# Rows of a batch turned for the queries: by a trip to DRAM and VectorE's 32x32 transposes, instead of TensorE

## The chip, the cores and the metric

The kernel runs on one core of a Trainium2 chip. A core has engines that each take their own instructions in order: TensorE (PE; its weight loads are shown apart as PEld), VectorE (DVE), ScalarE (ACT), GpSimd (POOL) and SyncE (SP), which here only issues DMAs. They wait for each other through semaphores. The metric is the device time of one execution in microseconds (us); it is given as a median of runs.

## The reference

One decoder layer in float32 over 16 sequences of 256 tokens with 256 channels, in three stages, each with a residual and a layer norm:

```python
x = _layernorm(x + _L0_attn_ref(x, w_fc, w_proj, ln_g, ln_b))        # squared-relu "attention" on fixed keys
x = _layernorm(x + _L0_xattn_ref(x, ctx, ctx, frac, Wq, bq, ...))    # 16 heads of 16, 256 keys
x = _layernorm(x + _L0_ffn_ref(x, gate_W, gate_b, wi_W, ...))        # top-1 of 8 LoRA experts
```

The change lies in the cross-attention of the second stage, in how its queries are made:

```python
Q = query @ Wq.T + bq ; K = key @ Wk.T + bk ; V = value @ Wv.T + bv
logits = einsum('bhqd,bhkd->bhqk', Q, K) * scale
D = clip(frac[:, None, :] - frac[:, :, None], -0.2, 0.2)
attn = gamma * logits + delta * (ap * max(D, 0) + an * min(D, 0))
out = softmax(attn) @ V @ Wo.T + bo
```

## The kernel before, in words

All instructions are put in an order by hand; no planner moves them, and each engine runs its share of them in that order.

The first stage runs over 8 blocks of 512 tokens (two batches each). It leaves normed rows in `hid`, a tile of 128 partitions (tokens) x 32 x 256 channels; `norm_out` writes a row block there (ScalarE, L245, then a GpSimd addition of `bo`, L413).

The second stage runs over 64 groups: group n is batch n // 4 and four of its heads. In the loop over n (L1068), group n's scores are made by TensorE (`logits`, L649) on top of a bias that ScalarE has put into the four PSUM banks (`positive`, L640); VectorE adds the other part of the bias and takes maxima (`maxima`, L664); GpSimd and VectorE subtract them (L679); one group later TensorE transposes the result (`Group.turned`, L689), ScalarE takes exponentials (L696), and two groups later TensorE multiplies with the values (`attend`, L705). Between these lie pieces for other batches, given by `pieces(n)` (L727): for n = 4b the queries of batch b+1 (L471), for 4b+1 the output projection of batch b-2 (L601), for 4b+2 the keys of batch b+1 (L497), for 4b+3 its values (L519), and then the small piece `ahead.turned()` for batch b+2. From group 15 on the third stage's blocks (L884, L896, L914) are woven in.

`Batch.turned` (L453) is the piece that the change rewrites. `hid` has tokens on partitions, and the query projection needs channels on partitions. So TensorE transposes the four 128x128 parts of a batch's rows into one PSUM tile (L458), and ScalarE copies it to `xT` (L465). `queries` then multiplies `wq` with `xT`. Batch 0 is turned in the last block of the first stage, batch 1 in group 0, and batch b+2 at the end of group 4b+3.

All DMAs of the second stage are issued by SP, in order. For one batch these are, with the group in which they stand: in group 4b+1 `gather` (L561 `sums`, then eight L569 `v`) for batch b-1; in 4b+2 the reciprocals' trip to DRAM (L579 `rows<-inv`), the eight DMAs that put batch b+1's keys in place (L513, `kM`: first four for heads of groups 4b+4 and 4b+6, then four for the other two) and the eight that spread the reciprocals (L587, `invs`); in 4b+3 loads of a later batch (L438 `cT` and L449, L451 or L442). The division (L594, `divide`) by `invs` is done on VectorE in group 4b+4.

`tile_b()` hands out PSUM tiles in the second stage from three banks in turn. `biases` (L139), in the second block of the first stage, subtracts from `bq` the product of `wq` with the vector `bo` that is added to the rows; it turns `bo` to columns with two TensorE transposes.

Of the kernel before, what the change touches and what calls it, by code (L numbers as in the profile page):

```python
# [14 lines left out]
P = 128  # L15
# [7 lines left out]
def tile_decoder_layer(ctx: ExitStack, tc: tile.TileContext, a: dict, out: bass.AP):  # L23
# [79 lines left out]
    gateb = const.tile([P, 4, E], FP, name="gateb")  # L103
    loraB = const.tile([P, F], FP, name="loraB")

    def load_cross():
        load = nc.sync.dma_start
        for t, n in ((vv, "vv"), (wk, "wkT"), (wv, "wvT"), (wq, "wqT")):
            load(out=t, in_=a[n].rearrange("(c p) f -> p c f", p=P))
        for t, n in ((bq, "bq"), (bk, "bk"), (fcol, "frac_cols")):  # L110
            load(out=t, in_=a[n])
        for t, n in (
            (bo, "bo"), (apos, "alpha_pos"), (aneg, "alpha_neg"), (gamma, "gamma"),
            (delta, "delta"),
        ):
            load(out=t, in_=a[n].to_broadcast(list(t.shape)))

        wo_view = a["woT"].rearrange("(o g i d) f -> i g d o f", o=CC, g=4, i=2)
        bv_view = a["bv"].rearrange("x (o g i d) -> i g d (x o)", o=CC, g=4, i=2)
        for i in range(2):  # L120
            for g in range(4):
                rows = slice(64 * i + 16 * g, 64 * i + 16 * g + 16)
                load(out=wo[rows], in_=wo_view[i, g])
                load(out=bvc[rows], in_=bv_view[i, g])
# [14 lines left out]
    def biases():  # L139


        spread = small.tile([P, CC, P], FP, tag="spread", bufs=1, name="spread")
        nc.vector.tensor_copy(spread, bvc.unsqueeze(2).to_broadcast([P, CC, P]))
        yield
        ps = tile_b()
        for c in range(CC):
            nc.tensor.matmul(
                ps[:, 0:C], lhsT=spread[:, c, :], rhs=wo[:, c, :], start=(c == 0), stop=(c == CC - 1)
            )
        nc.vector.tensor_tensor(bo, bo, ps[:, 0:C], ALU.add)  # L150
        yield
        ps = tile_b()
        for c in range(CC):
            nc.tensor.transpose(ps[:, c * P : (c + 1) * P], bo[:, c * P : (c + 1) * P], ident)
        columns = small.tile([P, CC, P], FP, tag="spread", bufs=1, name="columns")
        nc.vector.tensor_copy(columns.rearrange("p c f -> p (c f)"), ps[:, 0:C])
        yield
        ps = tile_b()
        for o in range(CC):
            for c in range(CC):  # L160
                nc.tensor.matmul(
                    ps[:, o * P : (o + 1) * P],
                    lhsT=wq[:, c, o * P : (o + 1) * P],
                    rhs=columns[:, c, :],
                    start=(c == 0),
                    stop=(c == CC - 1),
                )
        for o in range(CC):
            nc.vector.tensor_tensor(
                bq[:, o : o + 1], bq[:, o : o + 1], ps[:, o * P : o * P + 1], ALU.subtract  # L170
            )
        nc.vector.tensor_scalar(bq_s, bq, qscale, None, ALU.mult)
        yield
# [247 lines left out]
    if True:  # L421
# [8 lines left out]
        class Batch:  # L430
# [15 lines left out]
            def reload(self):  # L446
# [3 lines left out]
                self.dpos = p2.tile([P, 2, S], FP, tag="dpos", name="dpos")  # L450
                nc.sync.dma_start(out=self.dpos, in_=self.away["dpos"])  # L451

            def turned(self):  # L453
                b = self.b
                ps = tile_b()
                for c in range(CC):
                    for j in range(2):
                        nc.tensor.transpose(  # L458
                            ps[:, c * S + j * P : c * S + (j + 1) * P],
                            hid[:, 2 * b + j, c * P : (c + 1) * P],  # L460
                            ident,
                        )
                yield
                self.xT = p2.tile([P, CC, S], FP, tag="xT", bufs=1, name="xT")
                nc.scalar.copy(self.xT.rearrange("p c t -> p (c t)"), ps)  # L465

            def queries(self, vector=False):
                ps = tile_b()
# [258 lines left out]
        def pieces(n):  # L727

            b, og = divmod(n, 4)
            ahead, nxt, last, older = (  # L730
                batches[b + d] if 0 <= b + d < B else None for d in (2, 1, -1, -2)
            )
            if og == 0:
                return nxt and nxt.queries(n > 16 and n % 8 == 0), None, []
            later = nxt if nxt and nxt.b >= MADE else None
            if og == 1:
                return older and older.project(), None, [later and (lambda: later.clip("dneg"))]
            if og == 2:
                return nxt and nxt.keys(), None, [later and (lambda: later.clip("dpos"))]
            more = [ahead and ahead.load]  # L740
            if ahead:
                more.append(ahead.reload if ahead.b < MADE else ahead.fractions)
            return nxt and nxt.vals(), ahead and ahead.turned(), more
# [205 lines left out]
    with tc.manual_schedule():  # L949
# [23 lines left out]
        for tb in range(NB):  # L973
            now = rows_in[tb]
            steps = [[] for _ in range(8)]

            mv = small.tile([P, 8, 2], FP, tag="mv8", bufs=2, name="mv8")
            if tb in (0, 1, NB - 1):
                nc.vector.memset(mv, 0.0)

            if tb > 1:
                last = rows_in[tb - 2]
                last.mv = mv[:, 4:8]
                for jj in range(2):
                    steps[1 + jj].append(lambda jj=jj: last.measure_out(jj))
                for j in range(4 if tb + 1 == NB else 1):
                    steps[7 - j // 2].append(
                        lambda j=j, tb=tb: last.norm_out(by[tb], 4 + j, j, nc.gpsimd)
                    )
            if tb > 2:  # L990
                older = rows_in[tb - 3]
                for j in range(1, 4):
                    steps[j].append(
                        lambda j=j, tb=tb: older.norm_out(by[tb - 1], 4 + j, j, nc.gpsimd)
                    )
            turning = []
            if tb + 1 < NB:
                nxt = rows_in[tb + 1]
                nxt.mv = mv[:, 0:4]
                if tb:  # L1000
                    steps[0].append(nxt.load)
                for jj in range(2):
                    steps[3 + jj].append(lambda jj=jj: nxt.measure(jj))
                steps[6].append(lambda tb=tb: nxt.norm_in(by[tb]))
                turning.append(lambda: nxt.turn_in(0))
                if tb:
                    turning.append(rows_in[tb - 1].turn_rows)
                turning.append(lambda: nxt.turn_in(1))
            if tb + 1 < NB or tb > 1:
                steps[5].append(lambda tb=tb, mv=mv: scale(tb, mv))  # L1010
            if tb == 0:
                steps[0] += [load_cross]
                steps[2] += [load_ffn]
            if tb == 1:
                steps[0].append(scales)
                steps[4].append(clips[0][0].fractions)
                output = biases()
                for m in range(4):
                    steps[m + 2].append(lambda: next(output))
            for k, ((at, m), (batch, which)) in enumerate(zip(slots, clips)):  # L1020
                if at == tb:
                    if which == "dneg" and k + 2 < len(clips):
                        steps[m].append(clips[k + 2][0].fractions)
                    steps[m].append(lambda batch=batch, which=which: batch.clip(which))
            if tb + 2 == NB:
                steps[3].append(first.load)
                steps[5].append(batches[1].load)
            if tb + 1 == NB:
                steps[4] += [lambda: groups[0].negative(3)]
                for m, together in ((4, early[:2]), (7, early[2:3])):  # L1030
                    steps[m] += [lambda p=piece: step(p) for piece in together * 2]
            for m in range(8):
                c, n2 = divmod(m, 4)
                coming = []
                for n in (2 * n2, 2 * n2 + 1):
                    coming.append((now, c, n, now.scores(c, n)))
                for block, c, n, pr in behind:
                    block.values(c, n, pr)
                    if n == 7:
                        block.keep(c)  # L1040
                behind = coming
                for piece in steps[m]:
                    piece()
            for piece in turning:
                piece()
# [283 lines left out]
```

## Time and profile before

| | |
|---|---|
| time, median of 3 runs (lowest to highest) | 899.78 us (899.75 to 899.96) |
| span of the profiled execution, first to last instruction | 898.3 us |
| time of the profiled execution beyond its span | not recorded; the median stands 1.48 us above the span |
| mean granted TensorE clock | 0.998 |
| busy: TensorE / VectorE / ScalarE / GpSimd | 887.4 / 713.1 / 567.3 / 398.5 us |
| DMA queue of SP and its share of the 16 DMA engines | 43520 packets, 35.52 MB, 14.5% |
| first stage ends, second begins | about 254 us |

How to read it: an engine's busy share is a mean over stages with different limits. "idle <-X" behind a row names what ended the engine's idle time before it. In a timeline, the first two columns are start and duration in us. A start-to-start distance tells more of TensorE's use than a duration does, since successive matmuls overlap. DMA rows on SP (SPq) show the issue, not the transfer.

### The profile page before, as it was taken

Reading aid. Unit: us, or ns where it says so; the run is one execution under the profiler, and the core shown is the slowest. Engines: PE = TensorE matmul, PEld = TensorE weight load, DVE = VectorE, ACT = ScalarE, POOL = GpSimd, SP = SyncE. Lnnn points to the kernel's source line nnn. Section 1 sums busy time; section 2 is a strip of 40 time slices with the busy share of each in tenths; the row PEclk is TensorE's granted clock in tenths of the full one; section 3 lists DMA queues with packets and bytes.
Section 4 is the critical chain, followed back from the end, with each engine's and each line's share of the span. In section 5 each row is a group of like instructions: output and inputs, shape, how many; then the busy total and the mean of one; then the engine's idle time right before and its main releaser. Section 6 shows DMA issues by size and latency. Waiting matters only on the chain.

```text
span 898.3 us, 19061 instructions
## 1 busy us (share of the span) xinstructions
PE 887.4 (99%) x6940; PEld 560.8 (62%) x6940; DVE 713.1 (79%) x1986; ACT 567.3 (63%) x951; POOL 398.5 (44%) x385
## 2 busy tenths in 40 slices
PE   8999999999999999999999999999999999999997
PEld 4334444444466777577668757766875786586555
DVE  6879899988779999778777877877798787778344
ACT  5766777777787888376656836666684665556111
POOL 1100223422489998435534644563464456344010
PEclk9999999999999999999999999999999999999999
DMA  5501110110001222011111102011110201111001
GB/s 140 154 1 42 53 42 26 30 49 1 14 1 55 70 69 57 14 42 23 34 49 39 47 14 67 20 37 45 43 48 14 66 20 37 43 28 43 23 2 46
DMA packets 44190, 37.01 MB, mean 41 GB/s; under 512 B 14912, under 2 KB 40000, under 8 KB 44096
## 3 DMA queue, kind: packets, MB, share of 16 engines
q1 hardware_dynamic: 43520, 35.52, 14.5%
q8 instruction: 55, 0.90, 0.4%
q14 instruction: 39, 0.32, 0.1%
q10 hardware_dynamic: 576, 0.26, 0.1%
HBM read 21.07 MB, written 6.03 MB: 30 GB/s over the span
## 4 chain that ended last, share of the span: by engine, by line
PE 97%; DVE 1%; ACT 1%; issue 0%; POOL 0%; DVEq 0%; ACTq 0%; POOLq 0%
PE ps_b L689 13%; PE ps_a L339 13%; PE ps_v L358 12%; PE ps_l L884 12%; PE ps_l L649 8%; PE ps_b L914 7%; PE ps_v L705 7%; PE ps_v L914 5%; PE ps_b L601 3%; PE ps_b L497 3%; PE ps_b L471 3%; PE ps_b L519 3%; PE ps_l L896 2%; PE ps_b L811 1%; PE ps_b L458 1%; PE ps_b L796 1%
## 5 line engine op out<-in xcount | busy, mean ns | idle before, releaser
L628 POOL TENSOR_SCALAR neg<-dneg,aneg,delta 128x512 f32<-128x512 f32 x217 | 182.9, 854 | 181.8 <-PE ps_b L689 127.4
L664 DVE CUSTOM_DVE_ANT_0 neg<-ps_l,neg 128x256 f32<-128x256 f32 x512 | 181.5, 420 | 26.5 <-PE ps_l L649 22.6
L640 ACT ACTIVATE ps_l<-dpos,apos_d 128x512 f32<-128x512 f32 x256 | 172.9, 687 | 40.3 <-DVE mx L664 35.6
L696 ACT ACTIVATE pT<-ps_b 128x512 f32<-128x512 f32 x256 | 142.4, 591 | 59.3 <-PE ps_b L689 57.2
L348 DVE TENSOR_TENSOR pr<-pr 128x1024 f32<-128x1024 f32 x128 | 153.9, 1243 | 30.2 <-ACT pr L347 29.8
L347 ACT ACTIVATE pr<-ps_a 128x1024 f32<-128x1024 f32 x128 | 124.9, 1025 | 52.9 <-PE ps_a L339 52.5
L689 PE MATMUL ps_b<-ident,neg 128*128 128x128 f32 x1024 | 138.5, 277 | 2.0 <-ACT pT L696 1.8
L689 PEld LDWEIGHTS ps_b<-ident,neg 128*128 128x128 f32 x1024 | 113.6, 141 | 35.9 <-issue 12.4
L679 POOL TENSOR_TENSOR neg<-neg,mx 128x1024 f32<-128x1024 f32 x65 | 124.2, 1911 | 18.2 <-DVE mx L664 17.0
L339 PE MATMUL ps_a<-xnT,kT 64*64 64x512 f32 x1024 | 124.6, 593 | 1.0 <-ACT xnT L324 0.4
L358 PE MATMUL ps_v<-pr,vv 64*64 64x512 f32 x1024 | 122.7, 589 | 0.0
L884 PE MATMUL ps_l<-xt,wi 128*128 128x512 f32 x248 | 111.5, 595 | 0.0
L679 DVE TENSOR_TENSOR neg<-neg,mx 128x1024 f32<-128x1024 f32 x63 | 99.2, 1575 | 0.6
L413 POOL TENSOR_TENSOR hid<-hid,bo 128x256 f32<-128x256 f32 x32 | 43.7, 1367 | 105.3 <-ACT hid L245 86.5
L358 PEld LDWEIGHTS ps_v<-pr,vv 64*64 64x64 f32 x1024 | 45.2, 133 | 64.4 <-issue 54.5
L339 PEld LDWEIGHTS ps_a<-xnT,kT 64*64 64x64 f32 x1024 | 42.0, 133 | 65.2 <-issue 52.7
L649 PE MATMUL ps_l<-kM,qT 32*128 32x256 f32 x1024 | 75.9, 401 | 0.0
L884 PEld LDWEIGHTS ps_l<-xt,wi 128*128 128x128 f32 x248 | 45.3, 190 | 49.0 <-issue 44.4
L373 POOL TENSOR_TENSOR xt<-xt,half 128x512 f32<-128x512 f32 x15 | 19.1, 1273 | 120.3 <-ACT half L372 120.3
L914 PE MATMUL ps_b<-wof,hT 128*128 128x256 f32 x304 | 68.4, 380 | 0.0
L705 PE MATMUL ps_v<-pT,vaug 128*32 128x256 f32 x1024 | 66.4, 384 | 0.0
L907 DVE TENSOR_SCALAR hT<-ps_l,wib 128x512 f32<-128x512 f32 x43 | 29.8, 746 | 43.9 <-PE ps_l L896 43.9
(131 smaller groups left out, 1087.3 us busy)
## 6 DMA issues: line engine op xcount, KB each, us to landing
cT<-in_ctxT SPq DMA_DIRECT2D x16, 256.0 KB
kM<-keys SPq DMA_DIRECT2D x128, 32.0 KB
v<-raw SPq DMA_DIRECT2D x128, 32.0 KB
invs<-rows SPq DMA_DIRECT2D x128, 32.0 KB
x<-in_x SPq DMA_DIRECT2D x7, 512.0 KB
out<-x SPq DMA_DIRECT2D x7, 512.0 KB
frow<-in_frac SPq DMA_DIRECT2D x16, 128.0 KB
wi<-in_wiT SPq DMA_DIRECT2D x1, 1024.0 KB
```

Of the source, the lines that this page charges most:

```text
L339: nc.tensor.matmul(sc[64 * k : 64 * k + 64, h, :], lhsT=kT[64 * h : 64 * h + 64, q, hf * P + 64 * k : hf * P + 64 * k + 64], rhs=self.xnT[ ...
L348: nc.vector.tensor_tensor(pr, pr, pr, ALU.mult)
L358: nc.tensor.matmul(self.acc[k][64 * h : 64 * h + 64, :], lhsT=vv[64 * k : 64 * k + 64, hf, 64 * q : 64 * q + 64], rhs=pr[64 * k : 64 * k + ...
L628: nc.gpsimd.tensor_scalar(self.neg[:, g], self.batch.dneg, aneg[:, h : h + 1], delta, ALU.mult, ALU.mult,)
L640: nc.scalar.activation(banks[g], self.batch.dpos.rearrange("p j k -> p (j k)"), AF.Copy, scale=apos_d[:, h : h + 1],)
L649: nc.tensor.matmul(banks[g][:, j * S : (j + 1) * S], lhsT=self.batch.qT[rows, self.o, j * P : (j + 1) * P], rhs=self.batch.kM[rows, self.i ...
L664: nc.vector.tensor_tensor_reduce(out=self.t[:, g, j, :], in0=banks[g][:, j * S : (j + 1) * S], in1=self.neg[:, g, j, :], scale=1.0, scalar ...
L679: eng.tensor_tensor(rows, rows, top.to_broadcast([P, 4, S]), ALU.subtract)
L689: nc.tensor.transpose(ps[:, k * S + j * P : k * S + (j + 1) * P], self.t[:, g, j, k * P : (k + 1) * P], ident,)
L696: nc.scalar.activation(self.pT[:, g, :], self.ps[g], AF.Exp)
L884: nc.tensor.matmul(self.banks[g], lhsT=wi[:, c, f * P : (f + 1) * P], rhs=self.xT[:, c, :], start=(c == 0), stop=False,)
L914: nc.tensor.matmul(ps[:, 0:C], lhsT=self.hT[f][:, j * P : (j + 1) * P], rhs=wof[:, f, :], start=(f == 0), stop=(f == FC - 1),)
```

## The change

Three edits.

First, a new piece `Batch.regroup`, which issues five DMAs on SP. One stores a batch's 256 rows of 256 channels from `hid` to a DRAM tile. Four load them into `z`: partition 32q + r gets, of rows r, 32 + r, 64 + r ..., the 64 channels from 64q on, in pieces of 256 bytes. The piece stands at the end of group 4b+1 for batch b+2, after `gather` and before the reciprocals' store; for batches 0 and 1 in the seventh block of the first stage.

Second, `Batch.turned` has no TensorE or ScalarE work: after an empty first step, one VectorE transpose in blocks of 32x32 makes `xT` out of `z`, at the place where ScalarE's copy stood. With that, channel 64q + 32c + s lies on partition 32q + s, chunk c, instead of partition p and chunk c for channel 128c + p.

Third, the query weights are laid out in that order of channels (four DMAs in place of one), and `biases` brings `bo` into that order with one more VectorE copy (128x256).

```diff
+    def blocked(rows):
+        return rows.rearrange("p (q c s) -> p c q s", q=4, c=CC)
+
+    def load_blocked(t, name):
+        view = a[name].rearrange("(q c s) f -> q s c f", q=4, c=CC)
+        for q in range(4):
+            nc.sync.dma_start(out=t[32 * q : 32 * q + 32, :, 0 : view.shape[3]], in_=view[q])
+
     def load_cross():
         load = nc.sync.dma_start
-        for t, n in ((vv, "vv"), (wk, "wkT"), (wv, "wvT"), (wq, "wqT")):
+        for t, n in ((vv, "vv"), (wk, "wkT"), (wv, "wvT")):
             load(out=t, in_=a[n].rearrange("(c p) f -> p c f", p=P))
+        load_blocked(wq, "wqT")
...
         nc.vector.tensor_tensor(bo, bo, ps[:, 0:C], ALU.add)
+        mixed = small.tile([P, CC, P], FP, tag="spread", bufs=1, name="mixed")
+        nc.vector.tensor_copy(mixed.rearrange("p c (q s) -> p c q s", q=4), blocked(bo))
         yield
         ps = tile_b()
         for c in range(CC):
-            nc.tensor.transpose(ps[:, c * P : (c + 1) * P], bo[:, c * P : (c + 1) * P], ident)
+            nc.tensor.transpose(ps[:, c * P : (c + 1) * P], mixed[:, c], ident)
...
+            def regroup(self):
+                away = drams.tile([S, C], FP, tag="rows_in", name="away_h")
+                nc.sync.dma_start(
+                    out=away.rearrange("(j p) c -> p j c", p=P),
+                    in_=hid[:, 2 * self.b : 2 * self.b + 2, :],
+                )
+                self.z = p2.tile([P, 8, 2 * 32], FP, tag="z", name="z")
+                view = away.rearrange("(t r) (q v) -> q r t v", r=32, q=4)
+                for q in range(4):
+                    nc.sync.dma_start(out=self.z[32 * q : 32 * q + 32], in_=view[q])
+
             def turned(self):
-                b = self.b
-                ps = tile_b()
-                for c in range(CC):
-                    for j in range(2):
-                        nc.tensor.transpose(
-                            ps[:, c * S + j * P : c * S + (j + 1) * P],
-                            hid[:, 2 * b + j, c * P : (c + 1) * P],
-                            ident,
-                        )
                 yield
                 self.xT = p2.tile([P, CC, S], FP, tag="xT", bufs=1, name="xT")
-                nc.scalar.copy(self.xT.rearrange("p c t -> p (c t)"), ps)
+                nc.vector.transpose(
+                    self.xT.rearrange("p c (t r) -> p t c r", r=32),
+                    self.z.rearrange("p t (c s) -> p t c s", c=CC),
+                )
...
             if og == 1:
-                return older and older.project(), None, [later and (lambda: later.clip("dneg"))]
+                return older and older.project(), None, [
+                    later and (lambda: later.clip("dneg")), ahead and ahead.regroup,
+                ]
...
             if tb + 2 == NB:
+                steps[1].append(first.regroup)
                 steps[3].append(first.load)
                 steps[5].append(batches[1].load)
+                steps[6].append(batches[1].regroup)
```

## The prediction

> **What bounds the kernel now.** I read the page first, then the groups by line, then the stretches of time with each engine's busy share, and last the order of time on TensorE, VectorE and SP around the lines that the change touches. The first two lines below are the page's busy time and the engine part of its chain of waits.
>
> ```profile
> PE 887.4 (99%) x6940; PEld 560.8 (62%) x6940; DVE 713.1 (79%) x1986; ACT 567.3 (63%) x951; POOL 398.5 (44%) x385
> ...
> PE 97%; DVE 1%; ACT 1%; issue 0%; POOL 0%; DVEq 0%; ACTq 0%; POOLq 0%
> ```
>
> TensorE has work 99% of the span. The change takes work from it, so a gain is to be had, as long as TensorE is what ends last in each place. Groups by line, the two that go (L458, L465) and two that price the new one; the columns are busy us, mean ns of one, and the idle time before:
>
> ```profile
> L718 DVE COPY raw<-ps_v 128x512 f32<-128x512 f32 x32 | 21.9, 684 | 0.5 <-PE ps_v L705 0.5
> ...
> L209 DVE TENSOR_SCALAR x<-x,mv,rs 128x256 f32<-128x256 f32 x32 | 11.7, 420 | 0.4
> ...
> L458 PE MATMUL ps_b<-ident,hid 128*128 128x128 f32 x64 | 9.7, 275 | 0.0
> L465 ACT COPY xT<-ps_b 128x512 f32<-128x512 f32 x16 | 9.6, 600 | 0.4 <-PE ps_b L458 0.4
> ```
>
> The shares are means over stages, so I asked for stretches. The columns are length, then busy us of PE, PEld, DVE, ACT and POOL:
>
> ```profile
> 254.00:260.00 6.00, 6.00 (x52) 4.48 (x45) 5.82 (x23) 3.99 (x7) 3.72 (x3) 1.00 0.01 3
> ...
> 284.00:290.00 6.00, 5.05 (x60) 3.56 (x56) 6.00 (x20) 5.03 (x9) 5.70 (x6) 1.00 0.05 11
> 290.00:318.00 28.00, 27.94 (x265) 20.97 (x266) 25.27 (x96) 22.81 (x41) 26.02 (x25) 1.00 0.26 66
> ...
> 325.00:360.00 35.00, 35.00 (x327) 26.01 (x324) 34.20 (x114) 29.19 (x56) 31.75 (x31) 1.00 0.23 66
> ...
> 380.00:860.00 480.00, 480.00 (x3516) 340.76 (x3515) 373.22 (x1219) 286.99 (x520) 226.22 (x223) 1.00 0.14 37
> ```
>
> From 380 us on TensorE is full and VectorE 78%: TensorE's work is the time. Between 254 and 360 us (groups 0 to 16) VectorE is as full as TensorE, in places (5.82 of 6, 6.00 of 6, 34.20 of 35) fuller. Work moved from TensorE to VectorE gains in the one and costs in the other.
>
> **TensorE, removed.** In order of time:
>
> ```profile
> 394.33 1.04 PE L689 MATMUL ps_b<-ident,neg 128*128 128x128 f32 x8
> 395.20 0.60 PE L458 MATMUL ps_b<-ident,hid 128*128 128x128 f32 x4
> 395.73 1.15 PE L649 MATMUL ps_l<-kM,qT 32*128 32x256 f32 x16
> ```
>
> From the start of L689 to that of L649 are 1.40 us; where no L458 lies between, L689 to L649 takes 0.97 us (385.17 to 386.14). So four turns are worth 0.43 us, not the 0.60 us of their row; over 16 batches 7.0 us is the most that can be won.
>
> The ten batches 6 to 15 (groups 19, 23 ... 55) lie in the full stretch. In the five at groups 19, 27 ... the banks for the next scores are long ready: 0.43 x 5 = 2.2 us. In the other five ScalarE's last bias copy ends at 429.97 (429.26 + 0.71) and the scores start at 430.07; starting 0.43 us sooner their fourth product would wait some 0.1 us for it: 0.3 x 5 = 1.5 us. Batch 0 is turned in the first stage, TensorE-bound (99.95 of 100 us from 100 to 200 us): 0.45 us. Together -4.1 us.
>
> ScalarE's 16 copies (9.6 us) are worth nothing by themselves: after the one at 301.44 it sat idle 1.18 us. One PSUM bank less is asked for per batch; TensorE waits for such banks (1.8 us in 4 waits, its weight loads 4.0 us in 7, all behind the exponentials), so the bound is a gain of up to 1.8 us; I take 0, as half of them lie where VectorE is full.
>
> **VectorE, added.** No 32x32 transpose is in the trace. It moves 128x512 f32. From below: half the elements take 0.42 us (L209); from above, 128x1024 with two inputs takes 1.58 us (L679). Nearest is the 128x512 copy, 0.68 us by its row, 0.60 us from start to start; I take 0.65 us. From 380 us on it falls into VectorE's free 22%: 0 (were that cover gone, 0.65 x 10 = 6.5 us). Where VectorE is full it costs itself, and the 0.43 us is not won either: batch 1 (group 0, ahead of the first maxima at 254.79) and batch 2 (group 3, about 277.8) +0.5 each, batch 5 (group 15, ahead of the maxima at 352.16) +0.65. Together +1.65 us. The one copy added to the bias set-up (128x256, 0.35 us) lies in the first stage under TensorE: 0; else 0.35 us.
>
> [...] The 128x512 copy gives 0.65 us. [...]
>
> **SP, added: five issues and a round trip per batch.** The store of 256 KB and the four loads are put at the end of groups 1, 5, 9 ... SP issues in order, and the loads wait until the store has landed. In order of time on SP:
>
> ```profile
> 288.12 5.17 SPq L569 DMA_DIRECT2D v<-raw  x8
> 293.39 0.52 SPq L579 DMA_DIRECT2D rows<-inv  x1
> 294.71 6.13 SPq L513 DMA_DIRECT2D kM<-keys  x8
> 300.89 3.84 SPq L587 DMA_DIRECT2D invs<-rows  x8
> ...
> 371.77 5.13 SPq L569 DMA_DIRECT2D v<-raw  x8
> 384.83 0.33 SPq L579 DMA_DIRECT2D rows<-inv  x1
> ```
>
> The new issues stand between v<-raw and rows<-inv; behind them queue rows<-inv, the next batch's keys (kM), the spread of the reciprocals (invs), the context load. Price: a 256 KB store issued at 75.58 moved its last bytes at about 77.1; the 16 KB rows<-inv at 834.23 let the loads behind it go at 835.84, 0.3 us after its bytes. So 2.0 us from issue to release, then four loads at 0.47 us (invs, 3.84 / 8): 3.9 us. From below 1.6 + 4 x 0.40 = 3.2 us; from above, with the last load's landing in the way of the next, 5.5 us.
>
> From group 17 on the gap after v<-raw (7.9 us at 376.9, at least 4.8 us later, 495.0 to 499.82) covers it: 0; without that cover 0.5 to 2 us a batch. In groups 5 and 9 there is no gap. A load's bytes are usable some 2.0 us after its issue (last invs issued 839.0, its reader starts 840.98). Group 8's scores need the first four kM parts: issued from 297.9 instead of 294.71, the fourth at 299.8, there at 301.5 to 301.8, while TensorE wants it at 301.05 today: +0.5 us. The reciprocals then land at 308.4; VectorE's division (L594), today at 307.36, would be ready at 307.9: +0.5. Batch 3: +1.0 us. Group 9 the same: kM from 322.0 instead of 318.52, the fourth there at 325.7, wanted at 324.71: +0.9; the division +0.4. Batch 4: +1.3 us (its transpose hides in the first wait). Group 13: kM there at 350.0, wanted at 350.86: 0. Together +2.3 us; bounds -0.9 (both batches win 0.43) and, with 1.6 us more in groups 8 and 12 and 0.7 in 16, +6.2.
>
> The three more weight loads early on delay SP by 1.3 us with nothing waiting (it idles from 32.8 to 71.4): 0. Pieces of 256 bytes add some 8.4 MB to queues busy 14.5%: 0; the transposes come 1.5 us (batch 4) to 15 us after the loads are due.
>
> **The sum.** -4.1 + 1.65 + 2.3 = -0.15 us against the profiled span of 898.3, so 898.15; the median of the runs, 899.78, lies 1.48 us above that span, and I carry that over: 899.6 us. Changes under 0.2% (1.8 us) cannot well be told from none here.
>
> **Rivals.** (A) The crowded groups take it: kM has more slack than I give it, and VectorE's lateness or the freed PSUM bank is made good. For it: the waits for PSUM banks, and 2.4 us between fill (fourth part issued 296.6) and need of kM today. Against: VectorE's 6.00 of 6. If the SP part falls to its lower bound, -0.15 - 3.2 = -3.4: 896.4; if every batch wins, -7.0: 892.8. (B) The transpose is dear: at two passes of the copy's 0.60 us, 1.2 us, the three full places cost 1.65 us more and batches 3 and 4, no longer hidden, 0.55 each: 2.75, so 902.4 us. It decides for slower from about 1.05 us (five places x 0.4 us). For it: nothing in the trace but the longer rows; against it: the 128x512 rows lie near 0.68 us. (C) SP's round trip is at its upper bound, 5.5 us: 1.6 us more in groups 8 and 12, 0.7 in 16: +3.9, 903.5. For it: SP is busy nearly all the 24.3 us between two gathers there. Against: landings of 2.0 us.
>
> **The numbers.** Forecast (the parts cancel, 898.0 to 901.5) 0.37; A 0.32; B 0.18; C 0.13. Leaving out the last tenth of A and of B with C gives 894.3 to 905.5 (C's end and 2 us for what stands at 0 above). Faster by over 0.2% is A, 0.32; within it 0.37; slower B and C, 0.31.
>
> **What would show it.** Right: L458 gone; scores after group 19 some 0.4 us sooner each batch; 0.6 to 0.7 us for the transpose; VectorE without a gap before groups 0, 4, 16; SP's rows<-inv near 297.5; a TensorE gap at the scores of groups 8 and 12. Wrong: no such gap and an early 380 us mark (A), a transpose over 1 us (B), or kM later than 303 (C).

## The result and the profile after

The changed kernel takes 904.56 us (median of 5 runs, 904.46 to 905.41) against 899.78 us (5 runs by now, 899.64 to 899.96): a ratio of 1.0056, 95% interval 1.0045 to 1.0067. It is 0.56% slower by that ratio. The time lies inside the predicted range, but the likeliest case, that the parts cancel, did not come true; the profiled execution (904.55 us) has a span of 902.8 us where 898.15 was forecast. These are the lines of its page and of its groups by line that answer to those of before:

```profile
span 902.8 us, 19072 instructions
...
PE 889.7 (99%) x6876; PEld 557.8 (62%) x6876; DVE 723.3 (80%) x2003; ACT 560.7 (62%) x935; POOL 397.0 (44%) x385
...
PE 94%; DVE 2%; ACT 1%; issue 1%; DMA 1%; SPq 0%; DVEq 0%; ACTq 0%
```

```profile
L735 DVE COPY raw<-ps_v 128x512 f32<-128x512 f32 x32 | 21.9, 684 | 0.5 <-PE ps_v L722 0.5
L479 DVE STREAM_TRANSPOSE xT<-z 128x512 f32<-128x512 f32 x16 | 11.3, 705 | 0.0
```

TensorE has 64 instructions fewer and yet more busy time: short waits inside a run of products count as busy on the page. The scores' row shows it: 83.2 us busy on the page of the changed kernel against 75.9 before, with the same mean of one product (402 and 401 ns). TensorE's share of the chain fell from 97% to 94%, and DMA is in it now. The transpose costs what a copy of its size does, 0.70 us.

The stretches, with the same columns as before (length, busy us of PE, PEld, DVE, ACT and POOL; the last three are the granted clock of TensorE, the DMA share and GB/s):

```profile
254.00:260.00 6.00, 6.00 (x37) 4.22 (x37) 6.00 (x24) 2.83 (x5) 3.63 (x2) 1.00 0.01 3
...
290.00:318.00 28.00, 27.40 (x254) 19.75 (x251) 23.66 (x89) 20.50 (x36) 24.07 (x24) 1.00 0.30 80
...
325.00:360.00 35.00, 34.36 (x282) 23.92 (x280) 31.05 (x104) 24.27 (x46) 29.08 (x28) 0.95 0.28 72
...
380.00:860.00 480.00, 480.00 (x3477) 338.59 (x3476) 384.70 (x1243) 283.57 (x511) 227.82 (x225) 1.00 0.19 48
```

From 325 to 360 us VectorE went from 34.20 to 31.05 us although it had work added; TensorE, ScalarE and GpSimd did less too. All four engines wait for something else there. SP's order of time at the end of group 5, where the lateness begins, shows for what:

```profile
288.25 5.17 SPq L586 DMA_DIRECT2D v<-raw  x8
293.46 0.58 SPq L467 DMA_DIRECT2D away_h<-hid  x1
295.85 1.81 SPq L474 DMA_DIRECT2D z<-away_h  x4
297.76 0.40 SPq L596 DMA_DIRECT2D rows<-inv  x1
298.27 4.99 SPq L530 DMA_DIRECT2D kM<-keys  x8
303.31 4.77 SPq L604 DMA_DIRECT2D invs<-rows  x8
```

The store goes out at 293.46, its loads at 295.85 (they wait 1.8 us for the landing), and the reciprocals' store at 297.76: 4.3 us of trip. Everything behind is later: that store by 4.4 us (297.76 instead of 293.39), the keys by 3.6 (298.27 instead of 294.71), the spread of the reciprocals by 2.4 (303.31 instead of 300.89). TensorE's scores in groups 8 and 12, and VectorE's divisions in groups 8, 12 and 16 (order of time on each engine). Before:

```profile
301.05 1.15 PE L649 MATMUL ps_l<-kM,qT 32*128 32x256 f32 x16
...
324.71 1.15 PE L649 MATMUL ps_l<-kM,qT 32*128 32x256 f32 x16
```

```profile
307.36 0.68 DVE L594 TENSOR_TENSOR oT<-v,invs 128x512 f32<-128x512 f32 x1
...
331.21 0.68 DVE L594 TENSOR_TENSOR oT<-v,invs 128x512 f32<-128x512 f32 x1
...
357.91 0.68 DVE L594 TENSOR_TENSOR oT<-v,invs 128x512 f32<-128x512 f32 x1
```

In the changed kernel:

```profile
300.58 2.77 PE L666 MATMUL ps_l<-kM,qT 32*128 32x256 f32 x16
...
326.83 2.99 PE L666 MATMUL ps_l<-kM,qT 32*128 32x256 f32 x16 [0.52 <-DMA kM<-keys]
```

```profile
309.55 0.69 DVE L611 TENSOR_TENSOR oT<-v,invs 128x512 f32<-128x512 f32 x1 [1.83 <-DMA invs<-rows]
...
336.66 0.90 DVE L611 TENSOR_TENSOR oT<-v,invs 128x512 f32<-128x512 f32 x1 [2.47 <-DMA invs<-rows]
...
364.69 0.81 DVE L611 TENSOR_TENSOR oT<-v,invs 128x512 f32<-128x512 f32 x1 [1.23 <-DMA invs<-rows]
```

Sixteen products that take 1.15 us when fed take 2.77 and 2.99; the divisions come 2.19, 5.45 and 6.78 us later. The lateness is built in three steps, of 2.19, 3.26 and 1.33 us, each with waits for DMAs behind the trip. The loads themselves land hardly later: from the end of the last `invs` issue to the division that waits for it 1.47, 1.77 and 1.74 us pass in groups 8, 12 and 16, and 1.55 us at the division of before that waits (issue ends at 839.43, division at 840.98). In the waits by engine (total, times, longest), before and now:

```profile
DVE oT L594 <- DMA invs<-rows: 3.3, 1, 3.3
...
DVE oT L611 <- DMA invs<-rows: 9.4, 4, 3.9
```

One table serves for the result and the experiments. Ahead of a batch's `gather` SP waits for VectorE in this stretch (for `raw` 14 times, 181.2 us, in the whole profile of before), so its first DMA (`sums`) serves as a mark of how far the kernel is. The table gives its start minus that in the profile of before (287.36 in group 5, then 311.62, 335.87, 371.11, 567.07, and 828.42 for the last one), in us:

| kernel | group 5 | 9 | 13 | 17 | 37 | last | 5 to 17 | 17 to last |
|---|---|---|---|---|---|---|---|---|
| changed | 0.16 | 2.00 | 5.68 | 6.54 | 5.10 | 4.17 | +6.38 | -2.37 |
| trip earlier | 0.46 | 0.83 | 1.27 | 0.75 | -0.71 | -1.86 | +0.29 | -2.61 |
| trip alone | -0.51 | 1.50 | 4.15 | 4.28 | 4.28 | 4.28 | +4.79 | 0.00 |
| transpose alone | 0.42 | 0.53 | 0.50 | 1.04 | 1.24 | 1.22 | +0.62 | +0.18 |
| neither | -1.54 | -1.75 | -1.55 | -1.73 | -3.05 | -4.22 | -0.19 | -2.49 |
| no wait for landing | 0.12 | 0.57 | 2.95 | 3.52 | 2.07 | 1.08 | +3.40 | -2.44 |
| earlier, bank first | -0.29 | 0.49 | 0.81 | -0.04 | -1.71 | -2.85 | +0.25 | -2.81 |
| before, bank first | -1.13 | -1.14 | -1.13 | -0.76 | -0.01 | 1.02 | +0.37 | +1.78 |
| chosen by batch | -0.33 | -0.36 | -0.35 | 0.01 | -1.71 | -2.87 | +0.34 | -2.88 |
| earlier, copies shared | 0.54 | 1.01 | 1.44 | 0.82 | -0.20 | -1.22 | +0.28 | -2.04 |
| before, copies shared | -0.88 | -0.88 | -0.90 | -0.87 | -0.37 | 0.12 | +0.01 | +0.99 |

The two rows of "before" with an edit of the copies change nothing ahead of group 15, and still stand 0.9 and 1.1 us early in group 5. So the first columns differ by about 1 us between profiles for reasons outside these edits, and only differences along a row are read. The difference is there long before: ScalarE's first write of normed rows to `hid` stands at 97.97 us in the profile of before, at 96.81 and 97.10 in these two, at 97.69 in the changed kernel and at 97.60 with the transpose alone.

### The profile page after: what moved, and what is told of

Same layout as the page of the kernel before. It is cut to its first block, busy times and chain, and to the rows that moved or that the text cites. A ratio compares the mean times of both kernels' runs of the same rounds, so it can differ in the third digit from the quotient of the medians.

```text
span 902.8 us, 19072 instructions
## 1 busy us (share of the span) xinstructions
PE 889.7 (99%) x6876; PEld 557.8 (62%) x6876; DVE 723.3 (80%) x2003; ACT 560.7 (62%) x935; POOL 397.0 (44%) x385
## 4 chain that ended last, share of the span: by engine, by line
PE 94%; DVE 2%; ACT 1%; issue 1%; DMA 1%; SPq 0%; DVEq 0%; ACTq 0%
PE ps_b L706 13%; PE ps_a L351 12%; PE ps_v L370 12%; PE ps_l L903 12%; PE ps_l L666 8%; PE ps_b L933 7%; PE ps_v L722 7%; PE ps_v L933 5%; PE ps_b L514 3%; PE ps_b L618 3%; PE ps_b L488 3%; PE ps_b L536 2%; PE ps_l L915 2%; DVE neg L681 1%; PE ps_b L830 1%
## 5 line engine op out<-in xcount | busy, mean ns | idle before, releaser
L696 DVE TENSOR_TENSOR neg<-neg,mx 128x1024 f32<-128x1024 f32 x63 | 94.1, 1493 | 0.6
L666 PE MATMUL ps_l<-kM,qT 32*128 32x256 f32 x1024 | 83.2, 402 | 0.5 <-DMA kM<-keys 0.5
```

Of the source, the lines that this page charges most:

```text
L666: nc.tensor.matmul(banks[g][:, j * S : (j + 1) * S], lhsT=self.batch.qT[rows, self.o, j * P : (j + 1) * P], rhs=self.batch.kM[rows, self.i ...
L696: eng.tensor_tensor(rows, rows, top.to_broadcast([P, 4, S]), ALU.subtract)
```

## Experiments

My theory after the result (S): the trip itself is cheap; it costs because it stands in SP's queue ahead of the keys and reciprocals of a stretch (groups 5 to 16) in which SP has no gap from the gather to the last loads, and one of some 5 us behind them (306.22 to 311.62 before). Rivals: VectorE's transposes take the time (V), or the DMA traffic of the trip slows the transfers of others.

**The trip one group earlier.** SP's order at the end of group 4b has a gap. The piece goes there, behind the loads of group 4b-1 and ahead of the gather:

```diff
-                    later and (lambda: later.clip("dneg")), ahead and ahead.regroup,
+                    later and (lambda: later.clip("dneg")),
...
                 rows_in[NB - 1 - j // 4].norm_out(by[NB], j, j % 4, nc.gpsimd)
+            if n % 4 == 0 and n // 4 + 2 < B:
+                batches[n // 4 + 2].regroup()
```

> The changed kernel, with each batch's store and four loads issued at the end of group 4b instead of 4b+1: after the loads of group 4b-1 and ahead of the gather, where SP has about 5 us of nothing. Theory S (the round trip between the gather and rows<-inv delays kM and the reciprocals in groups 8 and 12; it cost some 5.5 us there): that cost goes, what stays is VectorE's transpose in full places, so 899.0 to 900.0 us. Theory V (VectorE's extra 0.70 us per batch is what costs): nothing is gained, 904 to 905 us.

Measured: 897.89 us (897.41 to 898.51) against 899.37 in the same session, ratio 0.9981 (0.9971 to 0.9990). Its SP timeline at the end of group 8, waits by engine, and the scores of groups 8 and 12:

```profile
306.58 0.43 SPq L467 DMA_DIRECT2D away_h<-hid  x1
310.56 1.80 SPq L474 DMA_DIRECT2D z<-away_h  x4
312.45 0.62 SPq L578 DMA_DIRECT2D sums<-raw  x1
313.12 5.51 SPq L586 DMA_DIRECT2D v<-raw  x8
318.74 0.52 SPq L596 DMA_DIRECT2D rows<-inv  x1
319.37 5.33 SPq L530 DMA_DIRECT2D kM<-keys  x8
```

```profile
DVE oT L611 <- DMA invs<-rows: 3.5, 1, 3.5
```

```profile
300.88 1.15 PE L666 MATMUL ps_l<-kM,qT 32*128 32x256 f32 x16
...
324.50 1.15 PE L666 MATMUL ps_l<-kM,qT 32*128 32x256 f32 x16
```

The same DMAs take longer here (4.0 us from the store to the first load, with three 256 KB loads just ahead of them), and yet `rows<-inv` follows `v<-raw` directly, the scores are back to 1.15 us, and of the waits for reciprocals only the one that was there before is left. From group 5 to 17 the kernel loses 0.29 us instead of 6.38: where the trip stands costs 6.1 us. The time is better than the theory's 899 to 900 us, and the change becomes a gain of 0.19%.

**The trip alone**, in the kernel before, at the place of the change; what it loads is not used, and TensorE still turns the rows.

```diff
+            def regroup(self):          # as in the change
...
-                return older and older.project(), None, [later and (lambda: later.clip("dneg"))]
+                return older and older.project(), None, [
+                    later and (lambda: later.clip("dneg")), ahead and ahead.regroup,
+                ]
...
+                steps[1].append(first.regroup)
                 steps[3].append(first.load)
                 steps[5].append(batches[1].load)
+                steps[6].append(batches[1].regroup)
```

> The kernel before, which still turns on TensorE, with the store and the four loads added at the places of the change; what they load is read by nothing. Theory S: slower by about as much as the changed kernel lost in groups 5 to 16, 5 to 6.5 us, so 904.8 to 906.3 us. Theory V: no change, 899.6 to 900.2 us.

Measured: 905.58 us (904.38 to 906.75, 4 runs), ratio 1.0068 (1.0053 to 1.0083). The waits of the profiled run:

```profile
DVE oT L605 <- DMA invs<-rows: 5.9, 4, 3.3
PEld ps_l L660 <- DMA kM<-keys: 2.7, 4, 1.9
```

Without any VectorE work added, the trip alone loses 4.79 us between groups 5 and 17, and nothing later. V is out as the main cause. Most of this lies in the same waits as in the changed kernel: VectorE for the reciprocals (5.9 us where it was 3.3), TensorE for the keys.

**The transpose alone**, in the kernel before: one more VectorE instruction per batch, from a constant tile into a spare one.

```diff
...
                 nc.scalar.copy(self.xT.rearrange("p c t -> p (c t)"), ps)
+                nc.vector.transpose(
+                    spare.rearrange("p c (t r) -> p t c r", r=32),
+                    zonce.rearrange("p t (c s) -> p t c s", c=CC),
+                )
```

> The kernel before, with one VectorE transpose added per batch at the place of the change, from a tile filled once into a tile that nothing reads; no DMA is added. Theory S: only the full places pay, groups 0, 3, 11 and 15 with up to 0.7 us each: 901.0 to 902.6 us. Theory V: 904 us or more.

Measured: 901.50 us (900.61 to 901.97), ratio 1.0021 (1.0012 to 1.0030), some 2 us. Of it 0.79 us lie between 98 us and group 5 (0.37 us ahead of before at 97.60, 0.42 behind it in group 5), where batches 0 to 2 are turned; 0.54 us between groups 13 and 17, where batch 5's transpose stands ahead of the maxima of group 16; from group 17 on 0.18 us. VectorE's free fifth covers the later ones as assumed. The trip alone and the transpose alone add up to 5.4 us between groups 5 and 17, where the changed kernel loses 6.38. The other 1.0 us lies between groups 9 and 13, where SP's issues of `v` and `invs` take 5.65 and 4.75 us, against 5.12 and 4.07 with the trip alone; why they do is open.

**Neither trip nor transpose**: the changed kernel with the queries made from a constant tile, so that only what TensorE and ScalarE lose is left.

```diff
...
-                self.xT = p2.tile([P, CC, S], FP, tag="xT", bufs=1, name="xT")
-                nc.vector.transpose(...)
+                self.xT = xonce
...
             def regroup(self):
+                self.z = zonce          # a constant tile in place of the five DMAs
```

> The changed kernel without the round trip and without the transpose: the queries of all batches are made from one constant tile, so the turning is left out. This bounds what any other way of turning can win. If TensorE's 0.43 us a batch is won everywhere: 892.9 us. If the five batches at groups 23, 31, 39, 47 and 55 win only 0.07 us, as in the changed kernel, and the four in groups where VectorE is full win nothing: 896.4 us.

Measured: 896.53 us (895.74 to 897.12), ratio 0.9967 (0.9954 to 0.9980). The turns are worth 3 us in all, not the 7.0 of their start-to-start cost. Between groups 5 and 17 three batches win 0.19 us together; from 17 on ten batches win 2.49 us.

**No wait for the landing**: the changed kernel, but the four loads read one DRAM tile that was stored once, with batch 0's rows. Same DMAs, same bytes, no wait of SP between the store and the loads; the queries are made from the wrong rows.

```diff
...
             def regroup(self):
+                if self.b == 0:
+                    once = drams.tile([S, C], FP, tag="once", bufs=1, name="once")
+                    nc.sync.dma_start(out=once.rearrange("(j p) c -> p j c", p=P), in_=hid[:, 0:2, :])
+                    fixed.append(once)
...
-                view = away.rearrange("(t r) (q v) -> q r t v", r=32, q=4)
+                view = fixed[0].rearrange("(t r) (q v) -> q r t v", r=32, q=4)
```

> The changed kernel at its own places, the same five issues and the same bytes, but the four loads read one DRAM tile stored once, so they don't wait for the store of the same group (the loaded rows are those of batch 0 for every batch; the dependence on the new rows is left out). Theory S1 (the wait for the landing, 1.8 us of the 4.3 us, is what exceeds the slack of kM, 2.4 us): most of the cost goes, 899.0 to 901.0 us. Theory S2 (the five issues and their 1024 pieces in the queues cost by themselves): 903 us or more.

Measured: 900.64 us (900.07 to 901.40), ratio 1.0012 (1.0002 to 1.0021), 4.0 us less than the change by the two ratios (0.44%). SP's order of time, and the division of group 8:

```profile
294.06 1.98 SPq L481 DMA_DIRECT2D z<-once  x4
296.15 0.38 SPq L603 DMA_DIRECT2D rows<-inv  x1
296.64 4.99 SPq L537 DMA_DIRECT2D kM<-keys  x8
301.69 4.89 SPq L611 DMA_DIRECT2D invs<-rows  x8
```

```profile
308.11 0.69 DVE L618 TENSOR_TENSOR oT<-v,invs 128x512 f32<-128x512 f32 x1 [0.56 <-DMA invs<-rows]
```

With the keys 1.6 us sooner, group 8 has lost almost all of its stall (0.45 us from group 5 to 9, against 1.84), and 5 to 17 costs 3.40 instead of 6.38 us. The DMA traffic is the same here, so these 3.0 us are SP's wait and not the traffic. By the two runs about half of the 6.1 us is the wait of 1.8 us, and half stays with the five issues (2.3 us), whose traffic this run doesn't part from their place in the queue; the landings above, 1.5 to 1.8 us with the trip and 1.55 without, speak against the traffic.

**Why half the later batches win nothing.** From group 17 on every version that takes the later turns from TensorE wins 2.0 to 2.9 us, where 3.7 was predicted. In the changed kernel the batches turned in groups 19, 27 ... win 0.43 us each, those in 23, 31 ... some 0.07. In the changed kernel's group 31, the scores on TensorE, and ScalarE's last bias copy behind its two copies of the block (second and third row):

```profile
514.44 1.51 PE L666 MATMUL ps_l<-kM,qT 32*128 32x256 f32 x16
```

```profile
513.11 1.07 ACT L818 COPY xt<-ps_b 128x512 f32<-128x512 f32 x2 [0.90 <-PE ps_b L815]
514.07 0.71 ACT L657 ACTIVATE ps_l<-dpos,apos_d 128x512 f32<-128x512 f32 x1
```

The bias copy ends at 514.78. The scores' fourth product wants it some 0.2 us after 514.44 (an estimate from 1.15 us for sixteen), and the sixteen take 1.51 us instead of 1.15. Three attempts to take that wait away:

*Bank first*: the bias copy ahead of the block's two copies, on top of the earlier trip, and alone in the kernel before.

```diff
-                ff.turn(nc.scalar.copy)
                 if nxt:
                     nxt.positive(3)
+                ff.turn(nc.scalar.copy)
```

> The early round trip of the first experiment, and ScalarE's fourth bias copy put ahead of its two copies of the block's transposed rows in groups 15, 23, 31, 39, 47 and 55. Theory (TensorE's scores wait there 0.36 us for that bank, which took the gain of five batches): 1.5 to 1.9 us less than the first experiment, 896.0 to 896.5 us. If something else holds these groups: no less, 897.9 us.

> The kernel before with that exchange of ScalarE's copies alone. Theory: TensorE reaches these scores 0.1 us or less before the bank is ready, so up to 0.5 us faster, 898.9 to 899.4 us. If the exchange gains by itself, it gains here as much as in the pair before it: 897.6 us.

Measured: 897.53 us (897.24 to 898.33), ratio 0.9978 (0.9969 to 0.9988), and 901.81 us (901.09 to 902.52), ratio 1.0026 (1.0016 to 1.0036). Both missed. TensorE's order of time in group 23 of the first of them:

```profile
428.97 0.66 PE L706 MATMUL ps_b<-ident,neg 128*128 128x128 f32 x4 [0.18 <-ACT xt L818]
429.56 1.15 PE L666 MATMUL ps_l<-kM,qT 32*128 32x256 f32 x16
```

The scores are fed again, but the block's copies, now later, free a PSUM tile too late for the transposes just ahead. The waits by engine between 380 and 830 us have this wait three times, 0.7 us in all, in groups 23, 39 and 47, and there the batches win nothing; in group 31 it does not show, and from group 29 to 33 the batch wins 0.39 us. In the kernel before, where nothing waited for the bank, the exchange costs 2.15 us from group 13 on.

*By batch*: batches 1 to 5, turned in the crowded stretch, stay on TensorE and ScalarE with a second copy of the query weights in the plain order; the others go by the earlier trip, with one buffer for `z` instead of two; bank first included.

```diff
...
             def turned(self):
+                if self.b in KEPT:                      # 1, 2, 3, 4, 5
+                    ps = tile_b()
+                    ...                                 # four TensorE transposes, as before
                 yield
                 self.xT = p2.tile([P, CC, S], FP, tag="xT", bufs=1, name="xT")
+                if self.b in KEPT:
+                    nc.scalar.copy(self.xT.rearrange("p c t -> p (c t)"), ps)
+                    return
...
-                            lhsT=wq[:, c, o * P : (o + 1) * P],
+                            lhsT=(wq_plain if self.b in KEPT else wq)[:, c, o * P : (o + 1) * P],
```

> Batches 1 to 5 turned on TensorE as before (with a second copy of the query weights in the plain order), the others by the early round trip and VectorE, and ScalarE's copies exchanged. Theory: nothing is lost in groups 0 to 16 (there the early round trip still cost about 0.8 us), batch 0 wins 0.5, the five at groups 19 to 51 win 0.43 each, the other five 0.3 to 0.43: 894.8 to 895.8 us. If VectorE's added time in full places costs nothing once the round trip is out of the way: no better than the kernel with the two edits, 896.2 us.

Measured: 897.35 us (896.84 to 897.91), ratio 0.9976 (0.9966 to 0.9985). It was expected to add the crowded stretch's saving to the rest, and missed: from group 5 to 17 it loses 0.34 us, as the version with all batches moved does (0.25).

*Copies shared*: ScalarE takes the block's first copy, VectorE the second; with the earlier trip, and alone in the kernel before.

```diff
-                    copy(self.xT[:, c, :], ps)
+                    (copy[c] if isinstance(copy, tuple) else copy)(self.xT[:, c, :], ps)
...
-                ff.turn(nc.scalar.copy)
+                ff.turn((nc.scalar.copy, nc.vector.tensor_copy))
```

> The version with the early round trip, and in the groups with a block's part 0 (15, 23, 31, 39, 47) the block's two copies out of PSUM are shared: ScalarE takes the first, VectorE the second, so that ScalarE's last bias copy, which the scores of the next group wait for, starts one copy (about 0.5 us) sooner and the PSUM tiles come free no later. Theory B (the five batches turned in groups 23, 31, 39, 47, 55 win only 0.07 us of 0.43 because that bias copy is late by 0.36 us): the wait goes, 0.3 us in each of the five groups, 1.5 us in all: 897.9 less 1.5, 896.0 to 896.8, and the 16 products of the scores there take 1.15 us in place of 1.51. Theory V (VectorE, which holds the scaled copy, the transpose and the maxima there, is the next to be late): the second copy (0.6 us on VectorE) delays the transpose and with it the queries, or the maxima; the wait moves from the scores to these and the time stays at 897.6 to 898.5.

> The kernel before with the same sharing of the block's two copies alone, TensorE still turning the rows. There the four turns give ScalarE's bias copy 0.43 us more and it ends 0.1 us before it is needed. Theory B: nothing is waited for that the sharing could remove, 899.2 to 899.8, no change; the gain of sharing comes only together with the change. Theory V: VectorE's extra copy delays its maxima: 0.2 to 0.4 us in five groups, 900.4 to 901.5. A time below 899 would say that ScalarE's order cost something before as well.

Measured: 898.58 us (897.96 to 899.16), ratio 0.9991 (0.9981 to 1.0000), and 900.52 us (900.21 to 901.19), ratio 1.0012 (1.0002 to 1.0021). The first is just past the upper end that theory V gave, far from theory B's; the second lies where V had it. In TensorE's order of time in the first, the scores of group 31 are fed (first row), and the transposes one group on wait for VectorE, which copies the queries out of PSUM late:

```profile
508.93 1.15 PE L666 MATMUL ps_l<-kM,qT 32*128 32x256 f32 x16
...
517.34 1.06 PE L706 MATMUL ps_b<-ident,neg 128*128 128x128 f32 x8 [0.42 <-DVE qT L499]
```

So theory V of that pair holds: in these groups ScalarE's bank, the PSUM tiles and VectorE are all within some tenths of a microsecond of being the next to be late. Taking one away brings the next in most of them. No version here makes all five batches win their 0.43 us.

## Why the prediction was wrong, by its own steps

**The sum.** Forecast were -0.15 us of span, measured +4.5 (902.8 against 898.3). By the table: before group 5 +0.16 us, of which -0.28 stand already at 98 us (97.69 against 97.97), so +0.44 from there on (predicted +0.55: batch 0 wins, batches 1 and 2 lose); groups 5 to 17 +6.38 us (predicted 2.3 + 0.65); from 17 to the last -2.37 us (predicted -3.7). 0.16 + 6.38 - 2.37 = 4.17; the last 0.3 us come behind the last gather, and what makes them is open. The 1.48 us from span to time, carried over, were some 0.3 us too few: in the eleven profiled runs with both on record the time lies 1.75 to 1.87 us above the span.

**The step that failed: SP's price, "Together +2.3 us".** Place and mechanism were right, and shown by moving the trip and by the trip alone. The trip's length was near: 3.9 us predicted, 4.3 measured. Too small was what the lateness does behind it: the place costs 6.1 us where 2.3 were forecast.

- Batch 3's keys: +0.5 predicted, +1.15 measured (the scores end at 303.35 instead of 302.20). Issue and landing were each a little later than taken (298.27, not 297.9; four issues of 0.62 us, and the loads of the last weights go on at 302.23), and when the fourth part is there most of the products are still to be done. I compared its landing with the start of the scores and counted nothing behind it.
- Batch 3's division: +0.5 predicted, +1.04 measured (2.19 in all). VectorE was ready at 307.7, as predicted (307.9); the reciprocals were there at 309.5, not 308.4. I priced their eight issues by one row of before, 3.84 us; they took 4.77, and the next two such rows of the old trace, which the prediction does not use, read 4.82 (at 323.57, the row below) and 5.34 (at 349.40).
- Batch 4: +0.9 and +0.4 predicted, +1.77 (329.82 against 325.86, less 2.19) and +1.49 measured.
- Batch 5 (group 16): no wait predicted, +0.89 measured at the scores (358.35 against 352.01, less 5.45) and +0.44 at the division. It stood among the upper bounds as "0.7 in 16".

```profile
323.57 4.82 SPq L587 DMA_DIRECT2D invs<-rows  x8
```

The upper bound of this term, 6.2 us, was reached with a trip of 4.3 us, not the 5.5 that I had tied to it. So rival C had the right engine and sign, and by its time (903.5) it came nearest, but its condition, a long trip, did not hold: the slack was smaller, not the trip longer. I took each wait from kind rows (3.84 us for eight issues, a landing set against the start of the scores); each was worth 0.4 to 1.1 us more, in a place where no engine has room to make it good, and there are six of them.

**TensorE's term, -4.1 us.** The five batches at groups 19, 27 ... win 0.43 us each, as predicted. The other five win 0.07, not 0.3: I saw ScalarE's bias copy there and gave it 0.1 us of delay. The bank is indeed some 0.12 us late in group 31 (514.78 against an estimated 514.66), but the sixteen products take 0.36 us longer; I left out what passes from ScalarE's end to TensorE's next product, an estimated 0.24 us. "Neither" shows the same loss without trip or transpose, so it belongs to the freed TensorE time itself.

**VectorE's term, +1.65 us.** The transpose was priced 0.65 us; it takes 0.70 and 0.62 from start to start (327.37 to 327.99). By the run with the transpose alone it costs 0.54 us for batch 5 (predicted 0.65) and 0.79 us up to group 5 for batches 0 to 2 (predicted 1.0). So this term held. Rival B is refuted by the row of 705 ns.

**Rival A** (the crowded groups take it) needed kM's slack of 2.4 us to cover most of the trip. It covers it only in group 8 and only when the wait for the landing is gone, as the run without it shows (its sixteen products there take 1.17 us, those of group 12 2.34).

**The signs listed.** L458 is gone; the transpose lies between 0.6 and 0.71 us; `rows<-inv` came at 297.76 where 297.5 was named; the scores of groups 8 and 12 are stretched. VectorE has no gap before group 0 (6.00 of 6). C's sign, keys later than 303, did not come: in group 8 the last weights load from 302.23. What was not foreseen is the wait in group 16.

## What to carry to other kernels

Where a DMA stands in an in-order queue can matter more than how long it takes: the same five DMAs cost 6 us ahead of other engines' inputs and next to nothing one group earlier, although they took longer there. Price a wait by everything that queues behind it until a gap in that queue, with the durations of several rows and not one, and count that each batch in a stretch without gaps pays again. Work taken from the bounding engine is won only as far as the next producer is early (here 0.43 us in each of five batches, 0.07 in the other five); where three engines run within tenths of a microsecond of each other, moving a copy mostly moved the wait (ratios of 0.9978 and 0.9991 with it, 0.9981 without).

## What the runs showed of the hardware beyond that

TensorE's granted clock fell in the profiled run of the changed kernel just behind the stalled scores of group 12. Stretches of 1 us; the last three columns are the granted clock, the DMA share and GB/s:

```profile
329.00:330.00 1.00, 1.00 (x16) 0.55 (x14) 0.41 (x3) 0.00 (x0) 1.00 (x2) 1.00 0.26 57
330.00:331.00 1.00, 1.00 (x16) 0.34 (x8) 1.00 (x9) 0.00 (x0) 0.34 (x1) 0.53 0.27 66
331.00:332.00 1.00, 1.00 (x8) 0.64 (x4) 1.00 (x7) 0.00 (x0) 0.79 (x1) 0.50 0.19 62
332.00:333.00 1.00, 1.00 (x7) 1.00 (x6) 0.97 (x5) 0.42 (x1) 1.00 (x1) 0.50 0.04 4
333.00:334.00 1.00, 1.00 (x6) 0.89 (x5) 1.00 (x1) 1.00 (x3) 0.11 (x1) 0.76 0.17 35
```

For 3.5 us ahead of it (326.32 to 329.82) TensorE had done work that takes 1.15 us when fed; then, in stretches of 0.25 us, the granted clock was 0.63 from 330.00, 0.50 from 330.25 to 333.25, 0.54 from there and 1.00 again from 333.50, and eight transposes from 331.37 took 1.97 us instead of 1.09. It cost nothing visible, as VectorE waited for reciprocals until 336.66 anyway, and runs of the changed kernel with a mean clock of 1.000 (905.41 us) are not faster than those at 0.997 (904.55). What makes the clock fall is not shown: the trip alone stalled in groups 8 and 12 too (its sixteen scores took 3.08 us from 300.54, and 3.64 us from 326.21 to 329.85), and the mean clock of its profiled run is 0.999.

The four runs of the trip alone lie in two pairs, 904.4 and 904.5 us (mean clock 0.999 and 1.000) and 906.7 and 906.8 us (both 0.996). Whether the clock makes that difference is open, since the changed kernel does not show it. A mean clock below 1 need not have cost anything: in the profile of before (0.998) it falls to 0.90 from 894 to 896 us and to 0.50 from 896 on, where TensorE has no work left.

Exchanging two copies on an engine that is 63% busy cost 2.3 us in the kernel before (901.81 against 899.52): an engine's share says nothing of how exactly its order is used.
